# Two-layer graph transformer on one core: the 20-token tile's matrix products in one accumulating group instead of four column quarters

## The chip, the cores and the metric

The kernel runs on one core of a Trainium2 chip. The metric is the device time of one execution in microseconds (us). TensorE is called PE in the profile, and its weight loads PEld; VectorE is DVE, ScalarE is ACT, GpSimd is POOL, SyncE is SP.

## The reference, cut to what matters

A graph of 2708 tokens with 512 features goes through two transformer layers. Attention is restricted to the neighbours of each token (a random symmetric graph with self loops), so each row of the 2708 x 2708 score matrix has at most some twenty live entries. All arithmetic is fp32.

```python
q = (h @ Wq.T + bq); k = (h @ Wk.T + bk); v = (h @ Wv.T + bv)      # 8 heads of 64
scores = einsum('nhd,mhd->hnm', q, k) / 8, -1e9 where there is no edge
ctx = einsum('hnm,mhd->nhd', softmax(scores), v).reshape(n, 512)
h1 = layer_norm(h + ctx @ Wo.T + bo)
h2 = layer_norm(h1 + relu(h1 @ W1.T + b1) @ W2.T + b2)             # 512 -> 2048 -> 512
```

## The kernel before, in words

The tokens are sorted by their number of neighbours and cut into 22 tiles of 128 tokens. 2708 is 21 x 128 + 20, so the last tile, number 21, has 20 tokens; the diff's names for its size are `r` (rows of a tile) and `size(g)`.

**Stages.** First `first` computes keys and values of layer 0 for all tiles and makes the neighbour lists on DVE (lines 832 to 901); `first_queries` computes the queries, ranks the tokens by neighbours (`ranked`, line 756) and starts the attention (lines 903 to 959). Then each layer runs its tiles in eleven blocks of two. Attention of a tile gathers the rows of its neighbours' keys and values by indirect DMAs from POOL (`loads`, L1004) and works on DVE and ACT. The feed-forward part of a block works on PE and ACT; the attention of the coming blocks is spread beside it by hand (`advance`, `through`). The blocks are the same for both layers:

```python
blocks = [(20, 19), (18, 17), (7, 9), (6, 10), (5, 11), (0, 16)]
blocks += [(1, 15), (2, 14), (3, 13), (4, 12), (NT - 1, 8)]
```

so the 20-token tile is the first member of the last block in each layer. Its partner, tile 8, is full.

**Order.** The instructions of PE, ACT and SP are issued in the order in which the program text makes them; DVE's order is by hand in `first_queries` and at the start of layer 1, POOL's in layer 0; elsewhere a scheduler chooses the order of DVE and POOL when the program is built.

**The products.** `project(xs, r, wm, name)` (line 566) multiplies a tile's 512 features with a 512 x 512 matrix: four chunks of 128 features, each with the tokens as the stationary operand (128 x r) and 512 columns of the matrix streaming. In fp32 every such product is two LDWEIGHTS and two MATMUL instructions, so a projection is eight of each. For a full tile the four chunks accumulate into one PSUM tile `o[:r]` (L576). For the 20-token tile (`r <= Q4`, Q4 = 32) they go to four different quarters of the PSUM partitions, 0 to 19, 32 to 51, 64 to 83 and 96 to 115 (L571); the four partial sums are then added up: the reader that evacuates PSUM takes quarter 0, and `plus_rest` (line 583) adds quarters 1 to 3 with one DVE instruction each (L586, or L588 where a scale is needed).

**The feed-forward part** (`Layer.feed_forward`, line 1311) walks 16 chunks `f` of the hidden width: `pf` (L1351) multiplies W1 with the tokens of both tiles (128 + 20 = 148 columns in the last block), ACT applies relu into `ft` (L1359), and three chunks later `second(f)` multiplies W2 with `ft` into the PSUM accumulators `a0`, `a1` of the two tiles (L1324). For the 20-token tile `second` does nothing; instead `quarters(f)` (line 1333, L1339) handles four chunks at a time, each into its own quarter of the accumulator. The ends of both tiles follow: residual add (L1375, then `plus_rest`), layer norm (`norm`, L1147 to L1160, with one POOL instruction L1156), and in layer 1 an indirect DMA to the output from POOL (L1379). In layer 0, `keys_values` (line 1390) then computes keys and values of layer 1 for both tiles and scatters them to DRAM (L1417), before layer 1 can gather them.

The very end: a product with one column, `pr` (L1647), forms a flag that all checks held; each engine loads the flag (L1663) and branches past a fall-back path.

Of the kernel before, what the change touches and what calls it, by code (L numbers as in the profile page):

```python
# [13 lines left out]
ALU = mybir.AluOpType  # L14
# [5 lines left out]
DM = 512  # L20
# [11 lines left out]
SAFE = 60.0  # L32
LIST = 24
SEG = 247
Q4 = 32

CAPS = (22, 14, 13, 12, 12, 11, 11, 10, 10, 9, 9, 9, 9, 8, 8, 8, 7, 7, 7, 6, 5, 3)
SLOTS = 2
# [434 lines left out]
def by_edges(ctx: ExitStack, tc: tile.TileContext, x, xT, adj, layers, out, good):  # L473
# [92 lines left out]
    def project(xs, r, wm, name, other=False):  # L566

        o = (ps_f if other else ps).tile([P, DM], F32, tag="f" if other else "g", name=name)
        if r <= Q4:
            for c in range(NC):  # L570
                nc.tensor.matmul(  # L571
                    o[c * Q4 : c * Q4 + r], xs(c), wm[:, c, :], start=True, stop=True
                )
            return o
        for c in range(NC):
            nc.tensor.matmul(o[:r], xs(c), wm[:, c, :], start=(c == 0), stop=(c == NC - 1))  # L576
        return o

    def rest(o, r):

        return [o[q * Q4 : q * Q4 + r] for q in range(1, 4)] if r <= Q4 else []

    def plus_rest(to, o, r, scale=None):
        for part in rest(o, r):
            if scale is None:
                nc.vector.tensor_tensor(to, part, to, ALU.add)  # L586
            else:
                nc.vector.scalar_tensor_tensor(to, part, scale, to, ALU.mult, ALU.add)  # L588

    def finish(steps):  # L590
        for _ in steps:
# [240 lines left out]
    def first(w, meanwhile):  # L832

        xg = []

        def load():
            i = len(xg)
            b = i % XBS * XB
            bw = min(XB, N - b)
            t = wts.tile([P, NC, XB], F32, tag=f"w1_{5 + i % 3}", name="xg")  # L840
            xg.append(t)
            step = bw if i else P
            for a in range(0, bw, step):
                nc.sync.dma_start(
                    out=t[:, :, a : a + step], in_=chunked(xT)[:, :, b + a : b + a + step]
                )
                yield

        def tokens(t, again):

            i, c0 = t * P // XB, t * P % XB
            if c0 == 0 and len(xg) < 2 * XBS:
                finish(load())
            xs = xg[i + again * XBS]
            return lambda c: xs[:, c, c0 : c0 + size(t)]

        wk = wts.tile([P, NC, DM], F32, tag="wk", name="wk")
        halves = load()
        next(halves)
        for c in range(NC):  # L860
            nc.sync.dma_start(out=wk[:, c, :], in_=chunked(w["Wk"])[:, c, :])
            if c == 0:
                cols = [given_column(w, "bk")]
        cols.append(given_column(w, "bq"))
        finish(halves)
        turning = turned_row(cols[0], "bk", 1.0)
        bk = next(turning)
        wv = matrix(w, "Wv", "wv")
        pa = tc.tile_pool(name="pa", bufs=2)
        lists, counted, ranked, listed = lists_of(pa.__enter__())  # L870
        done, before = 0, None
        for t in range(NT):
            r = size(t)
            xs = tokens(t, 0)
            kv = wts.tile([P, 2 * DM], F32, tag=f"w2_{5 + t % 3}", name="kvs")
            k = project(xs, r, wk, "k")
            if t == 0:
                finish(turning)
            nc.vector.tensor_tensor(kv[:r, :DM], k[:r], bk[:r], ALU.add)
            plus_rest(kv[:r, :DM], k, r)  # L880
            v = project(xs, r, wv, "v", other=True)
            nc.scalar.copy(kv[:r, DM:], v[:r])
            plus_rest(kv[:r, DM:], v, r)
            if before:
                nc.scalar.dma_start(**before)
            before = dict(out=kv_d[0][t * P : t * P + r, :], in_=kv[:r])
            if t == 0:
                finish(load())
            while done < min(NT, 1 + LEAD * t):
                lists(done)  # L890
                done += 1
                if done == NT:
                    counts = counted()
            meanwhile(t)
            if t == QT:
                wq = matrix(w, "Wq", "wq")
                turning = turned_row(cols[1], "bq", DK**-0.5)
                bq = next(turning)
                finish(turning)
        nc.scalar.dma_start(**before)  # L900
        return bq, wq, counts, ranked, listed, pa, tokens

    def first_queries(bq, wq, counts, ranked, listed, pa, tokens, meanwhile):
# [14 lines left out]
        for t in range(NT):  # L918
# [10 lines left out]
            nc.vector.scalar_tensor_tensor(  # L929
                qs[:r, t % 2], q[:r], DK**-0.5, bq[:r], ALU.mult, ALU.add  # L930
            )
            plus_rest(qs[:r, t % 2], q, r, DK**-0.5)
            if t == OWN - 1:
                listed(True)
                pa.__exit__(None, None, None)
# [36 lines left out]
    def own_query(g, zT, to, bq, wq):  # L972
# [1 line left out]
        r = size(g)  # L974
        q = project(lambda c: zT[:, c, :r], r, wq, "q")
        nc.vector.scalar_tensor_tensor(to[:r], q[:r], DK**-0.5, bq[:r], ALU.mult, ALU.add)
        plus_rest(to[:r], q, r, DK**-0.5)

    def checked():

# [194 lines left out]
    class Layer:  # L1175
# [83 lines left out]
        def query(self, g, zT):  # L1259
# [4 lines left out]
            nc.vector.scalar_tensor_tensor(  # L1264
                qs[:r], q[:r], DK**-0.5, self.bq[:r], ALU.mult, ALU.add
            )
            plus_rest(qs[:r], q, r, DK**-0.5)
            self.kept()
            self.due = (g, qs)

# [7 lines left out]
        def attended(self, block, got):  # L1278
# [11 lines left out]
            for g, r, cT, xb in cTs:  # L1290
                o = project(lambda c: cT[:, c, :r], r, self.wo, "o")
                h = dn.tile([P, DM], F32, tag="h", name="h", bufs=4)
                nc.vector.tensor_tensor(h[:r], o[:r], xb[:r], ALU.add)
                plus_rest(h[:r], o, r)
                if self.n == 0:
                    nc.vector.tensor_tensor(h[:r], h[:r], self.bo[:r], ALU.add)
                norm(h, r, self.g1, self.e1b2)
# [13 lines left out]
        def feed_forward(self, block, hs, hT):  # L1311
# [5 lines left out]
            def second(f, only=None):  # L1317
                c0 = 0
                for g, a in zip(block, accs):
                    r = size(g)  # L1320
                    if only not in (None, g) or r <= Q4:
                        c0 += r
                        continue
                    nc.tensor.matmul(  # L1324
# [3 lines left out]
                        start=(f == 0),  # L1328
                        stop=(f == NFC - 1),
                    )  # L1330
                    c0 += r

            def quarters(f):
                c0 = 0
                for g, a in zip(block, accs):
                    r = size(g)
                    for i in range(f - 3, f + 1) if r <= Q4 else ():
                        q = i % 4 * Q4
                        nc.tensor.matmul(  # L1339
                            a[q : q + r],  # L1340
                            fts[i][:, c0 : c0 + r],
                            self.w2[i // 2][:, i % 2, :],
                            start=(i < 4),
                            stop=(i >= NFC - 4),
                        )
                    c0 += r

            for f in range(NFC):
# [11 lines left out]
                fts.append(ft)  # L1360
                if f >= LAG:
                    second(f - LAG)
                if f % 4 == 3 and f < NFC - 1:
                    quarters(f)
                yield None
            for g in block:
                for f in range(NFC - LAG, NFC):
                    second(f, g)
                    if g == block[-1] and f == NFC - LAG:
                        quarters(NFC - 1)  # L1370
            zs = []
            for g, a, h in zip(block, accs, hs):
                r = size(g)
                z = h
                nc.vector.tensor_tensor(z[:r], a[:r], h[:r], ALU.add)  # L1375
                plus_rest(z[:r], a, r)
                norm(z, r, self.g2, self.e2)
                if self.n == NL - 1:
                    nc.gpsimd.indirect_dma_start(  # L1379
# [10 lines left out]
        def keys_values(self, block, zs):  # L1390
# [12 lines left out]
            for i, (g, z, zT) in enumerate(zip(block, zs, zTs)):  # L1403
# [1 line left out]
                kv = kvs[:, i, :]  # L1405
                k = project(lambda c: zT[:, c, :r], r, self.kv[0], "k")
                nc.vector.tensor_tensor(kv[:r, :DM], k[:r], self.bk[:r], ALU.add)
                plus_rest(kv[:r, :DM], k, r)
                v = project(lambda c: zT[:, c, :r], r, self.kv[1], "v")
                nc.scalar.copy(kv[:r, DM:], v[:r])  # L1410
                plus_rest(kv[:r, DM:], v, r)
                nc.sync.dma_start(out=zT_d[n][g], in_=zT)
                nc.sync.dma_start(out=xb_d[n][g * P : g * P + r, :], in_=z[:r])
                yield
# [292 lines left out]
```

## Time and profile before

| | |
|---|---|
| times of three runs | 1941.27, 1941.85, 1946.15 us; median 1941.85 |
| the profiled execution | 1946.15 us; its span 1944.3 us, 1.85 us of it outside the span |
| PE busy | 1858.4 us (96%), mean granted clock 0.981 |
| DVE / ACT / POOL busy | 1321.0 (68%) / 934.7 (48%) / 809.3 us (42%) |
| L1339, the quartered W2 products | 64 MATMULs, 8.4 us of PE, 600 ns mean of one |
| L1324, the other W2 products | 1344 MATMULs, 632.2 us of PE, 596 ns mean of one |
| L571, the quartered projections | 8 projections of 8 MATMULs |
| L586 and L588, the rest of the quarters | 30 DVE instructions, some 0.685 us each |

PE's busy time is the time in which at least one matmul runs, and matmuls overlap: a group's busy time is less than its count times its mean. Groups of one line with different shapes are told apart by their shapes: "128*20" is a stationary operand with 20 columns. In a timeline, the bracket behind a row says how long the engine sat idle before it, and what it waited for; "issue" means nothing that the profile shows. In a table of windows the columns are the window, its length, the busy time of PE, PEld, DVE, ACT and POOL with the number of instructions, the granted PE clock, the DMA share and GB/s. The times of day in the text are us from the span's start.

### The profile page before, as it was taken

The numbers are of one execution on the slowest core, as the hardware profiler recorded it, in microseconds if no ns is written. First come the engines' busy times: TensorE is split into PE (matmuls) and PEld (weight loads), VectorE is DVE, ScalarE is ACT, GpSimd is POOL, SyncE is SP. The second block draws the span as 40 slices with busy tenths as digits, with TensorE's granted clock in tenths as the row PEclk, the third lists the DMA queues.
The fourth block names the chain that finished last, engine by engine and source line by source line (L and its number), as shares of the span: only waits on it lengthen the run. The fifth ranks groups of instructions, "written<-read, shape, count | busy, mean of one in ns | idle before, by whom it ended". The sixth has DMA issues, their size and how long they took to land. (4 is left out here: it accounts for less than half of the span.)

```text
span 1944.3 us, 20898 instructions
## 1 busy us (share of the span) xinstructions
PE 1858.4 (96%) x6162; PEld 1096.7 (56%) x6162; DVE 1321.0 (68%) x2172; ACT 934.7 (48%) x3219; POOL 809.3 (42%) x710
## 2 busy tenths in 40 slices
PE   9998968999999999999999997999999999999996
PEld 4443435556656556665665553566666666666663
DVE  5885467768759687695841237696987998877421
ACT  4660236445546655574451113555475767654510
POOL 3113526535536555364410124344555775546101
PEclk9999979999999999999999998999999999999998
DMA  9998848555646656554401478656665766643000
GB/s 322 355 314 299 275 136 302 172 179 184 205 138 201 217 188 197 177 183 154 146 17 65 136 246 325 202 197 204 203 222 168 251 222 220 209 155 125 17 6 14
DMA packets 131486, 366.92 MB, mean 189 GB/s; under 512 B 16668, under 2 KB 37004, under 8 KB 128654
## 3 DMA queue, kind: packets, MB, share of 16 engines
q0 software_dynamic: 69120, 246.35, 38.0%
q1 hardware_dynamic: 53332, 99.66, 14.8%
q10 hardware_dynamic: 8910, 19.48, 2.6%
q8 instruction: 50, 0.82, 0.2%
q14 instruction: 74, 0.61, 0.1%
HBM read 314.62 MB, written 50.83 MB: 188 GB/s over the span
## 5 line engine op out<-in xcount | busy, mean ns | idle before, releaser
L1004 POOL DMA_INDIRECT kv<-kv_d,idx x420 | 547.0, 1302 | 452.2 <-DVE acc L1080 273.5
L1351 PE MATMUL pf<-hT,w 128*128 128x256 f32 (+1 forms) x2816 | 637.2, 373 | 7.2 <-ACT ft L1359 5.2
L1324 PE MATMUL a<-w,ft 128*128 128x512 f32 x1344 | 632.2, 596 | 5.3 <-ACT ft L1359 4.4
L1351 PEld LDWEIGHTS pf<-hT,w 128*128 128x128 f32 x2816 | 521.2, 191 | 186.6 <-issue 106.5
L1359 ACT ACTIVATE ft<-pf,b 128x256 f32<-128x256 f32 (+1 forms) x352 | 160.3, 460 | 458.5 <-PE pf L1351 458.3
L1041 DVE TENSOR_TENSOR kv<-kv,q 128x1024 f32<-128x1024 f32 (+3 forms) x222 | 254.2, 1157 | 169.2 <-DMA kv<-kv_d,idx 131.1
L1324 PEld LDWEIGHTS a<-w,ft 128*128 128x128 f32 x1344 | 253.2, 191 | 198.6 <-issue 171.6
L1067 ACT ACTIVATE kv<-kv,p 128x64 f32<-128x64 f32 x1232 | 311.0, 335 | 5.0
L1047 DVE TENSOR_REDUCE sc<-kv 128x16 f32<-128x1024 f32 (+3 forms) x222 | 253.8, 1153 | 1.5
L1080 DVE TENSOR_TENSOR acc<-acc,kv 128x1024 f32<-128x1024 f32 (+2 forms) x178 | 204.0, 1146 | 18.9 <-ACT kv L1067 17.0
L1156 POOL TENSOR_TENSOR rd<-va,mhalf 128x1 f32<-128x1 f32 (+1 forms) x88 | 90.4, 1028 | 274.6 <-DVE va L1154 273.7
L576 PE MATMUL o<-wo,cT 128*128 128x512 f32 x336 | 151.1, 602 | 0.5 <-ACT cT L1171 0.5
L1073 DVE TENSOR_TENSOR kv<-kv,p 128x512 f32<-128x512 f32 (+1 forms) x178 | 121.4, 682 | 34.6 <-ACT p L1060 34.6
L1060 ACT ACTIVATE p<-sc,minus 128x8 f32<-128x8 f32 x420 | 102.8, 294 | 69.2 <-DVE sc L1047 62.1
L1111 ACT ACTIVATE cx<-acc,su 128x64 f32<-128x64 f32 (+1 forms) x352 | 88.5, 334 | 74.7 <-DVE su L1103 57.6
L576 PEld LDWEIGHTS o<-wo,cT 128*128 128x128 f32 x336 | 64.5, 193 | 83.2 <-issue 72.9
L681 ACT ACTIVATE code<-aj 128x2708 bf16<-128x2708 int32 (+1 forms) x22 | 73.3, 3332 | 49.2 <-POOL aj L677 49.0
L684 DVE MAX8 tops<-code 128x8 f32<-128x247 f32 (+2 forms) x242 | 83.1, 401 | 19.3 <-ACT code L681 19.3
L1160 DVE SCALAR_TENSOR_TENSOR h<-h,rd,ln_b 128x512 f32<-128x512 f32 (+1 forms) x88 | 65.6, 747 | 40.6 <-POOL rd L1156 40.6
L1067 ACT ACTIVATE acc<-kv,p 128x64 f32<-128x64 f32 (+1 forms) x352 | 88.8, 334 | 1.4
L1410 ACT COPY kvs<-v 128x512 f32<-128x512 f32 (+1 forms) x22 | 12.9, 586 | 158.9 <-PE v L576 138.5
L1375 DVE TENSOR_TENSOR h<-a,h 128x512 f32<-128x512 f32 (+1 forms) x44 | 29.9, 679 | 85.2 <-PE a L1339 48.8
(154 smaller groups left out, 1560.2 us busy)
## 6 DMA issues: line engine op xcount, KB each, us to landing
aj<-in_adj SPq DMA_DIRECT2D x21, 1354.0 KB, 8.4
kv_d<-kvs ACTq DMA_DIRECT2D x21, 512.0 KB, 7.4
w<-in_W SPq DMA_DIRECT2D x20, 512.0 KB, 6.5
xg<-in_xT SPq DMA_DIRECT2D x19, 512.0 KB, 8.6
kv<-kv_d,idx POOLq DMA_INDIRECT x420, 5.8
w<-in_W ACTq DMA_DIRECT2D x12, 512.0 KB, 7.2
q_d<-qs SPq DMA_DIRECT2D x22, 256.0 KB, 3.4
zT_d<-zT SPq DMA_DIRECT2D x22, 256.0 KB, 4.3
```

Of the source, the lines that this page charges most:

```text
L576: nc.tensor.matmul(o[:r], xs(c), wm[:, c, :], start=(c == 0), stop=(c == NC - 1))
L1004: nc.gpsimd.indirect_dma_start(out=to, out_offset=None, in_=table[:, :], in_offset=bass.IndirectOffsetOnAxis(ap=s, axis=0), bounds_check=N ...
L1041: nc.vector.tensor_tensor(kv[:r, :c, :DM], kv[:r, :c, :DM], self.q[:r].unsqueeze(1).to_broadcast([r, c, DM]), ALU.mult,)
L1047: nc.vector.tensor_reduce(self.sc[:r, s0 : s0 + c, :], kv[:r, :c, :DM].rearrange("p s (h d) -> p s h d", d=DK), AX.X, ALU.add,)
L1060: nc.scalar.activation(p[:r, s, :], self.sc[:r, s, :], AF.Exp, bias=minus[:r, g, s : s + 1])
L1067: nc.scalar.activation(to[:, i, hd], kv[:r, i, DM + h * DK : DM + (h + 1) * DK], AF.Copy, scale=p[:r, s0 + i, h : h + 1],)
L1073: nc.vector.tensor_tensor(to[:, 0, :].rearrange("p (h d) -> p h d", d=DK), kv[:r, 0, DM:].rearrange("p (h d) -> p h d", d=DK), p[:r, s0, : ...
L1080: nc.vector.tensor_tensor(self.acc[:r, :c, :], self.acc[:r, :c, :], kv[:r, :c, DM:], ALU.add)
L1156: nc.gpsimd.tensor_tensor(rd[:r], va[:r], mhalf[:r], ALU.pow)
L1324: nc.tensor.matmul(a[:r], fts[f][:, c0 : c0 + r], self.w2[f // 2][:, f % 2, :], start=(f == 0), stop=(f == NFC - 1),)
L1351: nc.tensor.matmul(pf[:, :w], self.w1[f // 2][:, c, f % 2 * P : f % 2 * P + P], hT[:, c, :w], start=(c == 0), stop=(c == NC - 1),)
L1359: nc.scalar.activation(ft[:, :w], pf[:, :w], AF.Relu, bias=self.b1[:, f : f + 1])
```

## The change

The quarters go. `project` treats every tile as a full one: four chunks accumulate into `o[:r]`. `second` no longer skips the 20-token tile, so that per chunk `f` PE now does the W1 products of the block, two MATMULs with a 20-column stationary operand for tile 21, and two with 128 columns for tile 8. `quarters`, `rest`, `plus_rest` and their calls are removed. Blocks, tile order and loads stay as they are.

```diff
-Q4 = 32
 ...
     def project(xs, r, wm, name, other=False):
         o = (ps_f if other else ps).tile([P, DM], F32, tag="f" if other else "g", name=name)
-        if r <= Q4:
-            for c in range(NC):
-                nc.tensor.matmul(
-                    o[c * Q4 : c * Q4 + r], xs(c), wm[:, c, :], start=True, stop=True
-                )
-            return o
         for c in range(NC):
             nc.tensor.matmul(o[:r], xs(c), wm[:, c, :], start=(c == 0), stop=(c == NC - 1))
         return o
-
-    def rest(o, r):
-        return [o[q * Q4 : q * Q4 + r] for q in range(1, 4)] if r <= Q4 else []
-
-    def plus_rest(to, o, r, scale=None):
-        for part in rest(o, r):
-            if scale is None:
-                nc.vector.tensor_tensor(to, part, to, ALU.add)
-            else:
-                nc.vector.scalar_tensor_tensor(to, part, scale, to, ALU.mult, ALU.add)
 ...
             nc.vector.tensor_tensor(kv[:r, :DM], k[:r], bk[:r], ALU.add)
-            plus_rest(kv[:r, :DM], k, r)
             v = project(xs, r, wv, "v", other=True)
             nc.scalar.copy(kv[:r, DM:], v[:r])
-            plus_rest(kv[:r, DM:], v, r)
 ...            (the same in first_queries, own_query, query, attended, keys_values)
                 for g, a in zip(block, accs):
                     r = size(g)
-                    if only not in (None, g) or r <= Q4:
+                    if only not in (None, g):
                         c0 += r
                         continue
                     nc.tensor.matmul(
 ...
-            def quarters(f):
-                c0 = 0
-                for g, a in zip(block, accs):
-                    r = size(g)
-                    for i in range(f - 3, f + 1) if r <= Q4 else ():
-                        q = i % 4 * Q4
-                        nc.tensor.matmul(
-                            a[q : q + r],
-                            fts[i][:, c0 : c0 + r],
-                            self.w2[i // 2][:, i % 2, :],
-                            start=(i < 4),
-                            stop=(i >= NFC - 4),
-                        )
-                    c0 += r
 ...
                 if f >= LAG:
                     second(f - LAG)
-                if f % 4 == 3 and f < NFC - 1:
-                    quarters(f)
                 yield None
             for g in block:
                 for f in range(NFC - LAG, NFC):
                     second(f, g)
-                    if g == block[-1] and f == NFC - LAG:
-                        quarters(NFC - 1)
 ...
                 nc.vector.tensor_tensor(z[:r], a[:r], h[:r], ALU.add)
-                plus_rest(z[:r], a, r)
                 norm(z, r, self.g2, self.e2)
```

## The prediction

> **What bounds the kernel now.** I read first the table of windows around the places where the 20-token tile is worked on, to see where more PE time is more time.
>
> ```profile
> 150.00:175.00 25.00, 18.88 (x54) 8.24 (x53) 19.95 (x60) 1.75 (x3) 2.73 (x4) 0.86 0.91 319
> 275.00:300.00 25.00, 20.82 (x74) 13.10 (x73) 19.96 (x31) 11.62 (x46) 6.68 (x7) 0.86 0.38 114
> 1050.00:1075.00 25.00, 25.00 (x94) 15.18 (x93) 8.56 (x17) 4.88 (x15) 2.83 (x3) 1.00 0.05 22
> 1100.00:1125.00 25.00, 25.00 (x96) 13.56 (x94) 2.25 (x4) 4.41 (x13) 2.00 (x2) 1.00 0.80 258
> 1900.00:1925.00 25.00, 25.00 (x132) 15.23 (x131) 1.10 (x2) 4.22 (x11) 0.00 (x0) 1.00 0.00 1
> ```
>
> Both last blocks (1088 to 1137 and 1890 to 1926) run with PE busy for 25.00 of 25 us at clock 1.00, and DVE, ACT and POOL nearly idle: PE alone sets the time there, and nothing covers an added matmul. The first two rows are the other case: at the first keys and queries PE has idle time, and its clock fell (0.86).
>
> Next the timeline of weight loads in the last block, which prices the quarters.
>
> ```profile
> 1901.60 0.32 PEld L1324 LDWEIGHTS a<-w,ft 128*128 128x128 f32 x2
> 1902.16 0.19 PEld L1351 LDWEIGHTS pf<-hT,w 128*128 128x128 f32 x1 [0.24 <-issue]
> 1902.59 0.94 PEld L1351 LDWEIGHTS pf<-hT,w 128*128 128x128 f32 x7 [0.24 <-issue]
> 1903.47 0.32 PEld L1324 LDWEIGHTS a<-w,ft 128*128 128x128 f32 x2
> 1904.54 0.14 PEld L1339 LDWEIGHTS a<-w,ft 128*20 128x20 f32 x8 [0.76 <-issue]
> 1905.53 1.05 PEld L1351 LDWEIGHTS pf<-hT,w 128*128 128x128 f32 x8 [0.85 <-issue]
> 1906.52 0.32 PEld L1324 LDWEIGHTS a<-w,ft 128*128 128x128 f32 x2
> ...
> 1924.64 0.19 PEld L1324 LDWEIGHTS a<-w,ft 128*128 128x128 f32 x1 [0.24 <-issue]
> 1925.59 0.09 PEld L1647 LDWEIGHTS pr<-held,ones 128*1 128x1 f32 x2 [0.76 <-issue]
> ```
>
> A chunk without quarters takes 1903.47 - 1901.60 = 1.87 us, one with them 1906.52 - 1903.47 = 3.05: a group of eight quartered MATMULs (four chunks) costs 1.18. A 512-column MATMUL has a pitch of 0.43 us here (1902.59 - 1902.16). Eight in quarters are two passes of four side by side, 0.86; the other 0.32 is entering and leaving: the load before them waits 0.76 instead of 0.24, and the one behind them 0.85. The last row matters most: L1647 has no quarters, only a stationary operand of one column, and its load also waits 0.76. So what stalls PE is the change between wide and narrow operands, not the quartering.
>
> **The change part by part.** All differences are against this profile.
>
> W2 products of tile 21, per layer. Removed: 4 groups x 1.18 = 4.7 us. Added: 16 chunks x 2 = 32 MATMULs x 0.43 = 13.8. Per chunk they now stand between the W1 products and tile 8's, all 128 wide: one entry and exit for each of the 13 chunks in the loop and one for the last three together, 14 x 0.32 = 4.5. Net 13.8 + 4.5 - 4.7 = 13.6, for two layers **+27.2**. Bounds: with no stall for an uncrowded narrow operand 13.8 - 4.7 = 9.1 per layer; I take 0.32, because the L1647 row shows the stall. Nothing hides this.
>
> Projections. Each was 1.18 and becomes 8 x 0.43 + 0.32 = 3.76, +2.58. The two `o` projections (1064.2, 1868) lie in saturated PE: **+5.2**. The layer 1 query (1384.8) too, but PE later waits 2.0 and 0.6 us near 1632 and 1638, so 0 to 2.6; attention's ACT steps are queued behind the relu steps that PE feeds, so most of it carries on: **+1.8**. The keys and values between the layers are one quartered stretch from 1146.02 to 1147.94 = 1.92; they become 16 x 0.43 + 0.32 = 7.2, +5.3. They stand ahead of tile 8's keys and values, whose scatter (1156.05) the first gather of layer 1 waits for (1159.64), so it all counts, less 0.4 that tile 8's `v` now waits for `plus_rest` to free PSUM (load at 1151.44, idle 0.62 rather than 0.24): **+4.9**. The shorter layer norm ahead of it brings nothing: the two query projections that cover it keep PE busy to 1144.7.
>
> The first keys and values (154.2): PE then waits for DVE:
>
> ```profile
> 162.20 6.43 PE L576 MATMUL q<-wq,xg 128*128 128x512 f32 x8 [6.07 <-DVE kvs L879]
> 168.47 0.61 PE L763 MATMUL pr<-hot,tri 128*128 128x264 f32 x2
> ```
>
> Their +5.3 fits into the 6.07, at no cost; the PSUM that PE waits for isn't freed by the removed adds. But this idle time is also why the eight MATMULs after it run at half clock, 5.8 us from load to load where 3.5 is full speed. With 0.8 us of idle left the clock should hold (after a gap of 1.03 us at 1190 the pitch stayed 0.43), and the ranking behind them (L763, then 22 scatters on POOL, then the gathers, on which PE waits 14 us before 263) starts 2.3 earlier: **-2.3**, bounds 0 and -2.4. If the cover weren't there it would cost 5.3. The first query of tile 21 (276.2) goes into an idle 3.66 before 285.2, at no cost; that idle also halves the clock, and 32 MATMULs take 9.03 instead of 32 x 0.215 = 6.9: 0 to -2.1 there, mostly lost in PE's next waits for attention (1.97 and 2.86 us at 315 and 323): **-0.7**.
>
> DVE loses 30 instructions x 0.685 = 20.5 us. 27 of them lie beside saturated PE or in DVE's own waits: no gain, except that at 1384 DVE is nearly as full as PE (24.45 of 25), which is why the query's price above can fall to 0. The last three are in the tail, with POOL's scatters to the output behind them:
>
> ```profile
> 1929.21 2.18 POOL L1156 TENSOR_TENSOR rd<-va,mhalf 20x1 f32<-20x1 f32 x2 [32.06 <-DVE va L1154]
> 1931.96 1.16 POOL L1379 DMA_INDIRECT out<-h,ident_i  x1 [0.57 <-DVE h L1160]
> 1936.58 1.01 POOL L1379 DMA_INDIRECT out<-h,ident_i  x1 [3.47 <-issue]
> ```
>
> PE's last W2 MATMUL ends at 1925.66. Both norms run interleaved, tile 21's scatter starts 6.3 us later, and tile 8's waits until the first has landed (4.6 from start to start), though its rows were ready at 1932.3. In the new order tile 21's sums end 6 x 0.43 + 0.2 = 2.8 before tile 8's, and the add, statistics, POOL step and two scalings (0.69 + 0.69 + 0.3 + 1.3 + 0.75 = 3.7) let its scatter start some 1.3 after the end of PE instead of 6.3. The second follows 4.6 after, at 5.9 instead of 10.9: **-5.0**. The order of DVE and POOL is a scheduler's, so -2 (tile 21's last scaling behind all of tile 8's first steps) to -6.
>
> Sum: 27.2 + 5.2 + 1.8 + 4.9 - 2.3 - 0.7 - 5.0 = **+31.1**. The profiled execution (span 1944.3, 1946.15 in all) would become 1977.2; the median of the runs shown lies 4.3 lower, 1941.85, and becomes 1973.
>
> [...]
>
> **The rivals.**
> (a) No stall. If a lone 20-column operand at partition 0 counts as a full one, each term loses its 0.32s: W2 +18.2, `o` +4.5, query +1.5, transition +4.6, with the same early and late gains: 28.8 - 8.0 = +20.8, 1963. For: the quarters were the only 20-column products. Against: L1647, whose load is no quarter and waits as long. Chance 0.13.
> (b) No gains at the ends: clock, attention chain and scheduler give nothing back but 2 us of tail, and the query counts in full: 27.2 + 5.2 + 2.6 + 5.3 - 2 = +38.3, 1980. For: DMA is 0.8 to 0.9 busy at 150 to 250, so an earlier ranking may only wait for its gathers. Against: the gap of 0.8. Chance 0.17.
> (c) Faster. The added MATMULs are covered, as the first keys are, and the 20.5 us of DVE and the tail remain: -2.3 - 0.7 - 5.0 = -8, 1934. It needs some 31 us of PE idle in the two last blocks and the transition (it decides from there on); the windows show 25.00 of 25, and 24.83 at 1125. Chance 0.03.
> That the change doesn't do what its name says: the blocks are already in this order, and the diff moves none; only the quarters go, as costed.
>
> **How the numbers follow.** The forecast, 1973, has 0.67. The range takes in (a) at its low side with an early gain of 4 (1961) and (b) with a full-price transition (1980): 1961 to 1980. A measurement of this kernel tells 0.3%, some 6 us, from no change. Faster by more needs (c): 0.02. Within it: 0.02. Slower: 0.96.
>
> **What would show it.** In the new profile the "128*20" rows of L1324 should stand alone in pairs, each entered by a load that waited about 0.76, with a chunk of 1.87 + 0.86 + 0.32 = 3.05 us each time instead of every fourth time, and the last blocks 13.6 us longer. PE at 162 should run at a pitch of 0.43, and the two last scatters lie 1 and 6 us after PE's end. A chunk of 2.73 would be rival (a); a ranking that starts earlier with gathers that don't, rival (b). Idle PE inside the last blocks would make the whole sum wrong.

## The result, and the profile after

The changed kernel takes 1972.57 us (median of 4 runs, 1969.74 to 1974.75) where the kernel before, run beside it, takes 1943.05 (4 runs, 1941.27 to 1946.15): a ratio of 1.0149, 95% interval 1.013 to 1.0169, or 29.5 us slower. Run once more beside another set of runs of before (below), it took 1972.87 against 1941.06: ratio 1.0161, interval 1.0146 to 1.0176, 31.8 us slower. The forecast was 1973.0, from a sum of +31.1.

Its profiled execution took 1974.75 us, span 1972.9, mean granted clock 0.989 (before: 1946.15, 1944.3, 0.981). PE is busy for 1896.1 us, 37.7 more than before; DVE for 1302.7, 18.3 less. The table of windows at the places that the prediction used (the last one moved along with the last block; columns: window, length, busy us of PE, PEld, DVE, ACT, POOL with the number of instructions, granted clock, DMA share, GB/s):

```profile
150.00:175.00 25.00, 24.01 (x60) 9.53 (x60) 16.27 (x55) 1.16 (x2) 4.32 (x6) 1.00 0.92 309
275.00:300.00 25.00, 23.15 (x84) 14.64 (x83) 17.78 (x29) 15.89 (x62) 10.81 (x11) 1.00 0.55 171
1050.00:1075.00 25.00, 25.00 (x84) 13.93 (x83) 7.48 (x14) 4.18 (x13) 1.87 (x2) 1.00 0.00 0
1100.00:1125.00 25.00, 25.00 (x80) 11.93 (x79) 2.25 (x4) 2.70 (x6) 2.00 (x2) 1.00 0.76 246
1925.00:1950.00 25.00, 25.00 (x101) 12.61 (x99) 0.00 (x0) 3.43 (x9) 0.00 (x0) 1.00 0.00 1
```

The last blocks are still 25.00 of 25 for PE at clock 1.00, so nothing covered the added products. In the last row PE issues 101 matmuls in 25 us instead of 132. Over the whole kernel both versions issue 6162; tile 21's no longer run side by side in quarters (where a group of eight took 1.05 us before, at 1904.54), so the same number takes longer. At 150 and 275 PE's idle time is mostly filled and the clock is 1.00 where it was 0.86.

The timeline of weight loads in the last block of layer 1, from one chunk's load for tile 8 to the next:

```profile
1932.26 0.30 PEld L1300 LDWEIGHTS a<-w,ft 128*128 128x128 f32 x2 [0.85 <-issue]
1932.80 0.19 PEld L1312 LDWEIGHTS pf<-hT,w 128*128 128x128 f32 x1 [0.24 <-issue]
1933.23 0.94 PEld L1312 LDWEIGHTS pf<-hT,w 128*128 128x128 f32 x7 [0.24 <-issue]
1934.32 0.12 PEld L1300 LDWEIGHTS a<-w,ft 128*20 128x20 f32 x2 [0.15 <-issue]
1935.29 0.30 PEld L1300 LDWEIGHTS a<-w,ft 128*128 128x128 f32 x2 [0.85 <-issue]
```

From one load for tile 8 to the next, 1935.29 - 1932.26 = 3.03 us, in every chunk of the loop; before, it was 1.87 in three of four and 3.05 in the fourth. The pair of tile 21 (128*20) stands alone between W1's products and tile 8's. The load behind it waits 0.85, the one into it only 0.15.

The timeline of PE at the first query projection, and POOL's rows at the very end:

```profile
162.73 3.70 PE L569 MATMUL q<-wq,xg 128*128 128x512 f32 x8 [0.94 <-DVE kvs L861]
166.27 0.61 PE L745 MATMUL pr<-hot,tri 128*128 128x264 f32 x2
```

```profile
1959.24 0.93 POOL L1134 TENSOR_TENSOR rd<-va,mhalf 20x1 f32<-20x1 f32 x1 [40.97 <-DVE va L1132]
1961.27 0.95 POOL L1335 DMA_INDIRECT out<-h,ident_i  x1 [1.10 <-DVE h L1138]
1962.84 0.92 POOL L1134 TENSOR_TENSOR rd<-va,mhalf 128x1 f32<-128x1 f32 x1 [0.62 <-DVE va L1132]
1964.84 1.03 POOL L1335 DMA_INDIRECT out<-h,ident_i  x1 [1.08 <-DVE h L1138]
```

The idle time ahead of the query fell from 6.07 to 0.94, and its eight MATMULs now take 3.54 us from the first to the ranking's first (166.27 - 162.73; before 6.27). At the end, the last W2 MATMUL ends at 1960.04; the two scatters start 1.23 and 4.80 us later (before: 6.3 and 10.9), and the second now waits for its own rows on DVE, not for the first to land.

**Where the 28.6 us of the two spans lie.** I set the starts of the same PE rows in both traces side by side; each line is the growth of one stretch.

| stretch | before | after | difference |
|---|---|---|---|
| start to the block before the last of layer 0 (its first `pf`) | 1012.42 | 1005.16 | -7.3 |
| that block, with `o` of the last block beside it | 76.20 | 78.75 | +2.55 |
| last block, layer 0: first `pf` to the first query of layer 1 | 49.19 | 62.44 | +13.25 |
| from there to tile 8's keys | 10.14 | 14.88 | +4.7 |
| tile 8's keys to block 2 of layer 1 | 227.55 | 229.49 | +1.9 |
| block 2 of layer 1, with tile 21's query | 68.43 | 70.98 | +2.55 |
| blocks 3 to 8 of layer 1 | 385.40 | 386.20 | +0.8 |
| block 9, with `o` of the last block beside it | 61.59 | 64.14 | +2.55 |
| last block, layer 1: first `pf` to the last MATMUL's end | 34.74 | 48.00 | +13.25 |
| tail: from there to the end of the span | 18.67 | 12.89 | -5.8 |

Those that lie in saturated PE, and the tail, come to 2.55 + 13.25 + 4.7 + 2.55 + 2.55 + 13.25 - 5.8 = +33.05 us, 33.1 before rounding. The remaining three (-7.3, +1.9, +0.8) are -4.6 in this execution, and they are the ones that differ from kernel to kernel: block 1 of layer 1 (part of the +1.9 row), which no edit here touches, takes 71.9 us before and 74.0 in the kernel below whose only edit is at the very end. The first row differs as much where its code is the same: 1012.42 before, and 1008.39, 1013.26 and 1007.33 in the three kernels below that keep it as it was (independent scatters, W2 alone, early quarters). With the early products plain it is 1005.16 here and 1001.49 to 1006.68 in four more traces. So it is shorter after the change, by 5.8 us on average, but the 7.3 of one pair of executions is not its size.

### The profile page after: what moved, and what is told of

It reads as the page before. It is cut to its first block, busy times and chain, and to the rows that moved or that the text cites. A ratio compares the mean times of both kernels' runs of the same rounds, so it can differ in the third digit from the quotient of the medians.

```text
span 1972.9 us, 20865 instructions
## 1 busy us (share of the span) xinstructions
PE 1896.1 (96%) x6162; PEld 1103.9 (56%) x6162; DVE 1302.7 (66%) x2142; ACT 933.7 (47%) x3219; POOL 816.1 (41%) x710
## 5 line engine op out<-in xcount | busy, mean ns | idle before, releaser
L982 POOL DMA_INDIRECT kv<-kv_d,idx x420 | 556.6, 1325 | 446.3 <-DVE acc L1058 267.2
L1300 PE MATMUL a<-w,ft 128*128 128x512 f32 (+1 forms) x1408 | 661.9, 595 | 10.5 <-ACT ft L1320 7.5
L1300 PEld LDWEIGHTS a<-w,ft 128*128 128x128 f32 (+1 forms) x1408 | 255.7, 186 | 231.1 <-issue 196.2
L1058 DVE TENSOR_TENSOR acc<-acc,kv 128x1024 f32<-128x1024 f32 (+2 forms) x178 | 204.0, 1146 | 18.3 <-ACT kv L1045 16.3
L569 PE MATMUL o<-wo,cT 128*128 128x512 f32 (+1 forms) x352 | 157.4, 600 | 0.5 <-ACT cT L1149 0.5
L1051 DVE TENSOR_TENSOR kv<-kv,p 128x512 f32<-128x512 f32 (+1 forms) x178 | 121.5, 683 | 35.2 <-ACT p L1038 35.2
L569 PEld LDWEIGHTS o<-wo,cT 128*128 128x128 f32 (+1 forms) x352 | 65.9, 189 | 88.0 <-issue 77.5
L1371 POOL DMA_INDIRECT kv_d<-kvs,ident_i x22 | 24.7, 1121 | 157.6 <-ACT kvs L1365 78.3
```

Of the source, the lines that this page charges most:

```text
L982: nc.gpsimd.indirect_dma_start(out=to, out_offset=None, in_=table[:, :], in_offset=bass.IndirectOffsetOnAxis(ap=s, axis=0), bounds_check=N ...
L1051: nc.vector.tensor_tensor(to[:, 0, :].rearrange("p (h d) -> p h d", d=DK), kv[:r, 0, DM:].rearrange("p (h d) -> p h d", d=DK), p[:r, s0, : ...
L1058: nc.vector.tensor_tensor(self.acc[:r, :c, :], self.acc[:r, :c, :], kv[:r, :c, DM:], ALU.add)
L1300: nc.tensor.matmul(a[:r], fts[f][:, c0 : c0 + r], self.w2[f // 2][:, f % 2, :], start=(f == 0), stop=(f == NFC - 1),)
```

## Experiments

Two of the changed kernel's traits are on trial first, the price of a width change and the early gain; then the tail, then whether the terms add up, and last a version that might beat both. Stretches and tails below are measured as in the table above.

**The width change: tile 21's W2 products with a stationary operand of 128 columns.** The MATMULs are as many and as long, but no operand is narrow (the rows beyond the 20 tokens are never read).

```diff
-                        a[:r],
-                        fts[f][:, c0 : c0 + r],
+                        a,
+                        fts[f][:, c0 : c0 + P],
```

> The changed kernel, but tile 21's W2 products load all 128 columns that lie in ft (its own 20 and the first 108 of tile 8's, whose rows of the sum nobody reads): as many MATMULs of as many columns, none of them narrow. Theory (entering and leaving narrow operands stalls PE): a chunk of the last block falls from 3.03 to 2.73 us (1.87 + 2 x 0.43), the 14 changes per layer at some 0.3 go, 4.2 us per layer and 8.5 in all: about 21 us above the kernel before, 1964. Rival (streaming the 32 more MATMULs is the whole price, the waiting loads are only drawn that way): a chunk stays at 3.03 and the time at 29 above, 1972. Second rival (the wider load costs more than the narrow one saves): above 1972.

Measured: 1969.19 us, ratio to before 1.0125 (1.0101 to 1.0149), by the medians 23.0 us above before where 21 was expected; single runs spread from 1960.05 to 1973.02, so the blocks are the sharper measure. The two last blocks take 58.18 and 43.74, 4.25 less in each than after the change. The timeline of its weight loads:

```profile
1916.19 0.32 PEld L1300 LDWEIGHTS a<-w,ft 128*128 128x128 f32 x2
1916.74 0.19 PEld L1300 LDWEIGHTS a<-w,ft 128*128 128x128 f32 x1 [0.24 <-issue]
1917.17 0.19 PEld L1300 LDWEIGHTS a<-w,ft 128*128 128x128 f32 x1 [0.24 <-issue]
1917.60 0.19 PEld L1312 LDWEIGHTS pf<-hT,w 128*128 128x128 f32 x1 [0.24 <-issue]
...
1918.91 0.32 PEld L1300 LDWEIGHTS a<-w,ft 128*128 128x128 f32 x2
```

No load in the loop waits longer than 0.24, and a chunk takes 2.72 us, 0.31 less than with the narrow pair. A matmul on 128 columns of which 108 are thrown away is cheaper here than one on 20. 4.25 / 14 = 0.304 us for each entry with its exit.

**The same, by number of changes: tile 21's W2 products gathered in groups of four chunks,** in one accumulating group, so that each layer has 4 entries instead of 14.

```diff
-                    if only not in (None, g):
+                    if only not in (None, g) or r < P:
...
+                if f % 4 == 3 and f < NFC - 1:
+                    fours(f)        # four chunks' pairs of tile 21 in a row, into a[:r]
```

> The changed kernel, but tile 21's W2 products wait for four chunks and then run as eight narrow MATMULs in a row into one group, where the quarters stood: 4 changes of width per layer instead of 14. Theory (stall per change): 10 x 0.3 x 2 = 6 us below the changed kernel, about 23 above the kernel before, 1966, with one chunk in four at 1.87 + 3.44 + 0.3 = 5.6 us and the others at 1.87. Rival (price per MATMUL): 29 above, 1972.

Measured: 1967.77 us, ratio 1.0115 (1.0079 to 1.0152); the last blocks take 59.40 and 44.95, 3.05 less in each, which is 10 x 0.305. Its weight loads around a group (five equal rows left out):

```profile
1922.89 0.32 PEld L1300 LDWEIGHTS a<-w,ft 128*128 128x128 f32 x2
1923.96 0.12 PEld L1313 LDWEIGHTS a<-w,ft 128*20 128x20 f32 x2 [0.76 <-issue]
1924.41 0.10 PEld L1313 LDWEIGHTS a<-w,ft 128*20 128x20 f32 x1 [0.33 <-issue]
...
1927.50 1.05 PEld L1324 LDWEIGHTS pf<-hT,w 128*128 128x128 f32 x8 [0.85 <-issue]
```

Two different edits give the same price, 0.304 and 0.305, each by the number of changes that it takes away. Within the group the narrow loads follow each other at the ordinary pitch of 0.43: it is the change that costs, not the narrow operand.

**The clock gap alone: the kernel before, with 12 MATMULs that nobody reads in the 6.07 us ahead of the first query.** Quarters and adds all stay.

```diff
+            if t == NT - 1:
+                o = ps_f.tile([P, DM], F32, tag="f", name="warm")
+                for c in range(6):
+                    nc.tensor.matmul(o[:r], xs(c % NC), wv[:, c % NC, :], start=True, stop=True)
```

> The kernel before with its quarters, its rests and all its sums, and twelve idle MATMULs (20 columns wide, a result that nobody reads) put behind tile 21's first values, where PE stood idle for 6.07 us. Theory (the idle gap halved the clock of what follows): the first query's eight MATMULs run at a pitch of 0.43 instead of 0.85, the ranking starts about 2.3 us earlier, and with later waits that it shortens the whole is 2 to 5 us below the kernel before, 1938 to 1941. Rival (the changed kernel's early gain came from the removed DVE instructions): the pitch is 0.43, but the ranking's first scatter and the time stay as they were, 1943.

Measured: 1942.19 us, ratio 0.9994 (0.9972 to 1.0016). PE there:

```profile
154.99 5.31 PE L887 MATMUL warm<-wv,xg 128*20 128x512 f32 x12
160.24 3.70 PE L576 MATMUL q<-wq,xg 128*128 128x512 f32 x8
163.78 0.61 PE L763 MATMUL pr<-hot,tri 128*128 128x264 f32 x2
```

The query's eight MATMULs take 3.54 us instead of 6.27 with nothing changed but the idle time ahead of them, so that idle time is what had slowed them. The ranking's scatters start at 167.92 instead of 171.85, so the rival's sign, scatters that stay where they were, did not come. What this is worth at the end of the kernel (4.0 us less by the medians, 0.06% by the ratio), the interval can tell neither from nothing nor from the 2 to 5 us that were expected.

**The clock gap by the change itself: the kernel before, only tile 21's first keys and values out of the quarters,** with their six adds on DVE gone.

```diff
-            k = project(xs, r, wk, "k")
+            k = project(xs, r, wk, "k", plain=True)
...
-            plus_rest(kv[:r, :DM], k, r)
-            v = project(xs, r, wv, "v", other=True)
+            v = project(xs, r, wv, "v", other=True, plain=True)
...
-            plus_rest(kv[:r, DM:], v, r)
```

> The kernel before, with only tile 21's first keys and values (layer 0) in one accumulating group and without their rests; all else in quarters. Theory (clock): as with idle MATMULs in the gap, the ranking 2.3 us earlier, 2 to 5 us below the kernel before, and the same as that run within 1 us. Rival (the six removed DVE instructions count): 2 to 4 us below the run with idle MATMULs. Second rival (5.3 us more of PE reach the end, no cover): 1948.

Measured: 1944.19 us, ratio 0.9994 (0.9977 to 1.0012). From its timeline of PE:

```profile
161.60 3.70 PE L576 MATMUL q<-wq,xg 128*128 128x512 f32 x8
165.14 0.61 PE L763 MATMUL pr<-hot,tri 128*128 128x264 f32 x2
...
208.28 4.60 PE L576 MATMUL q<-wq,xg 128*128 128x512 f32 x5 [3.43 <-DMA xg<-in_xT]
```

The first pitch is as in the fill (3.54 us), and the ranking's scatters start at 168.53. Then PE waits 3.43 us at 208 for a load of token features, which in the profiled execution of before had come in time, and the first feed-forward block starts 4.1 later than before. A wait for that load also stands in the traces of the wide variant (1.36 us), of the groups of four (1.60) and of two kernels below (1.56 and 3.65), one of which still has the quarters there; in others it is absent. The time lies level with the fill's by the ratio and 2.0 us above it by the medians, so the rival's 2 to 4 below it, for the six adds, isn't borne out; nor is the second rival's 5 us over before, a ratio of 1.0026. So an early start can be lost to a transfer, and whether it is differs between kernels of equal code at that place.

**The early gain in the whole change: the changed kernel again, beside a variant that keeps the quarters of layer 0's first keys, values and query.** The variant is the changed kernel with the quarters' branch of `project` and `plus_rest` back for those three calls.

```diff
-    def project(xs, r, wm, name, other=False):
+    def project(xs, r, wm, name, other=False, plain=False):    # plain=True in all later calls
+        if r <= Q4 and not plain:                             # quarters, as before
...
+            plus_rest(kv[:r, :DM], k, r)
+            plus_rest(kv[:r, DM:], v, r)
+            plus_rest(qs[:r, t % 2], q, r, DK**-0.5)
```

> The changed kernel once more, unaltered, beside a variant that keeps the quarters at the beginning alone. What is open: the profiled execution of the changed kernel had 7.3 us of early gain (everything up to 1060 us came that much earlier) where the forecast had 3.0. Its stretches that lie in saturated PE, and its tail, add up to 26.6 + 5.0 + 2.6 + 4.6 - 5.8 = +33.0 us; what the time stays below that is the early gain. Theory of the forecast: an early gain of about 3, ratio 1.0154. Rival, 7.3 is what the change brings every time: ratio 1.0132. Third, no early gain that lasts: ratio 1.0170.

> The changed kernel, but with the quarters (and their adds) kept for the 20-token tile's first keys, values and query of layer 0, which lie beside idle PE. It pays all of the price, +33.0 us, and has none of what an early plain projection can bring: ratio to before 1.0170 by the theory that the clock gap at the first queries gives something, with the changed kernel 3 us below it (forecast) or 7.3 us below it (the profiled execution). Rival: what is gained there is lost in the waits for the gathers; then both variants take the same time to within 1.5 us, and any spread at 200 to 300 us is one of transfers that varies from execution to execution.

Measured, side by side: the changed kernel 1972.87 us (1971.99 to 1975.41), ratio 1.0161 (1.0146 to 1.0176); with the early quarters 1976.27 (1974.08 to 1980.04), ratio 1.0186 (1.017 to 1.0202). The difference of the medians is 3.4 us, near the forecast's 3.0, but the two intervals overlap. The rival of 7.3 every time (ratio 1.0132) lies below the changed kernel's interval here, though just inside that of the first comparison (1.013 to 1.0169). The third, no gain that lasts (1.0170), lies inside the interval here, and two variants at most 1.5 us apart aren't excluded either. With the early quarters the kernel stands 35.2 above before, where the fixed terms made 33; that is the lower end of its interval. The two profiled executions don't show where the 3.4 lie: at the start of block 2 of layer 0 they stand at 444.04 and 444.65.

**The tail: the changed kernel with tile 8's three last chunks ahead of tile 21's.**

```diff
-            for g in block:
+            for g in reversed(block) if w < 2 * P else block:
                 for f in range(NFC - LAG, NFC):
                     second(f, g)
```

> The changed kernel with one order turned round: in the last block the three products that are left over at the end come first for tile 8, then for tile 21. PE's work is the same. Theory (the tail became shorter because tile 21's sums end 2.8 us before PE's end, so that its norm runs beside PE): now tile 21's chain starts at PE's end, its scatter to the output starts some 4.0 us after that end instead of 1.2, the second scatter 7.5 to 8.6 after, and the time from PE's end to the span's end is 15.6 to 16.7 us instead of 12.9. Rival (only the three removed additions shortened the tail): it stays at 12.9, give or take 0.7.

Measured, in one run: 1977.54 us, tail 17.91 us (1957.80 to 1975.71). POOL at its end:

```profile
1960.24 2.18 POOL L1134 TENSOR_TENSOR rd<-va,mhalf 20x1 f32<-20x1 f32 x2 [44.02 <-DVE va L1132]
1963.00 1.16 POOL L1335 DMA_INDIRECT out<-h,ident_i  x1 [0.58 <-DVE h L1138]
1967.95 1.00 POOL L1335 DMA_INDIRECT out<-h,ident_i  x1 [3.80 <-issue]
```

The direction is the theory's, the size is beyond it (15.6 to 16.7 expected): with both sums ready at nearly the same time, the two norms run interleaved again (POOL's two steps stand in one row, "x2"), as before the change, so the first scatter starts 5.2 after PE's end, and the second waits for it. 17.91 - 12.89 = 5.0 us of the 5.8 is the order of the two sums, and 18.67 - 17.91 = 0.8 is left for the three adds. That rest isn't shown: two kernels that keep the adds and the old order (the first keys and values alone, the later fills alone) have tails of 17.96 and 17.70.

**The wait between the two last scatters: the kernel before, with the two scatters to the output declared independent** (they write different tokens' rows).

```diff
+                    tc.declare_no_dep(put.ins, group="put", reason="every token has one place")
+                    tc.add_to_no_dep_group("put", put.ins)
```

> The kernel before, with the two last scatters to the output (tile 21, then tile 8, different rows) declared independent of each other, so that POOL doesn't wait for the first to land before it starts the second. Theory: that landing is what the second scatter waited for (its rows were ready at the first one's start), so it starts 7.5 to 8 us after PE's end instead of 10.9, and the time from PE's end to the span's end falls from 18.7 to 15.3-15.8 us. Rival: it waited for something else on POOL or in the queue, and nothing moves: 18.7.

Measured, in one run: 1940.02 us, tail 15.55 us (1922.73 to 1938.28).

```profile
1929.03 1.15 POOL L1379 DMA_INDIRECT out<-h,ident_i  x1 [0.57 <-DVE h L1160]
1930.49 1.00 POOL L1379 DMA_INDIRECT out<-h,ident_i  x1 [0.30 <-issue]
```

The second starts 7.76 after PE's end, the idle time ahead of it is 0.30 instead of 3.47, and the tail is 3.1 shorter: the second scatter had waited for the first to land.

**W2 alone: the kernel before, with only tile 21's W2 products out of the quarters.** All its projections stay quartered.

```diff
-                    if only not in (None, g) or r <= Q4:
+                    if only not in (None, g):
...
-                    quarters(f)
...
-                        quarters(NFC - 1)
...
-                plus_rest(z[:r], a, r)
```

> The kernel before with only the W2 products of tile 21 taken out of the quarters (and with them their three residual adds per layer); all projections stay quartered. What is put on trial is whether the terms of the sum add up, and how much the early gain is worth. Theory: the last block of each layer grows by the 13.3 us that the trace after showed (49.2 to 62.5 and 34.7 to 48.0), the tail falls to 12.9 as after, so the profiled span lies 26.6 - 5.8 = 20.8 us above that of before, apart from the scatter of the first 1000 us. Against the changed kernel, the projections (2 x 2.5 for o, 2.55 for the query, 4.6 for keys and values, 12.2 in all) are missing and so is the early gain G that came with plain first keys and values: ratio to before 1.0107 in any case; the changed kernel's 1.0149 stands above it by 12.2 - G, that is 8.2 us with G = 4. Rival: the early gain is worth all of the 7.3 us that the profiled execution showed; then the two kernels lie only 4.9 us apart and the ratio here is 1.0124 or more. Third: there is no early gain at all: 12.2 us apart, ratio 1.0086 or less.

Measured: 1966.57 us, ratio 1.0121 (1.0092 to 1.015). In its trace the last blocks take 62.45 and 48.01 and the tail 12.72, as in the full change; the stretches with `o` grow by 0.0 in both layers, and the one with tile 21's query by -0.1. So the terms are separate and add up where PE is saturated. On the early gain the run is no judge: its interval holds the theory's 1.0107 and the rival's 1.0124, and misses only the third (1.0086), and by little.

**Filling three gaps and freeing the tail: the kernel before with its quarters,** the fill at the first query, the independent scatters, and 13 and 6 calls of a product that nobody reads in PE's gaps of 14.2 us (layer 0) and 7.4 us (layer 1) ahead of `o`; and, to tell its parts apart, the two later fills by themselves.

```diff
                 flip(cx, r, cT[:, :, :r], self.bv)
+                if g == order[0]:
+                    o = ps_f.tile([P, DM], F32, tag="f", name="warm")
+                    for c in range((13, 6)[self.n]):
+                        nc.tensor.matmul(o, ones, self.wo[:, c % NC, :], start=True, stop=True)
```

> A version meant to beat the kernel before: its quarters all stay, the two last scatters are independent, and PE's idle time is filled with products that nobody reads at three places (six calls in the 6.07 us gap at the first queries, 13 calls in the 14.2 us gap of layer 0 between the two transpositions of block 0's attended, 6 in the 7.4 us gap of layer 1), so that the clock isn't halved behind them. Theory: -3.3 in the tail, -5 where the clock stays full behind the two later gaps (o and the first W1 products of a layer at a pitch of 0.43 instead of 0.85), 0 to -3 from the first gap: -8 to -11, ratio 0.995 to 0.996. Rival (what is gained early and in the middle is lost in the next wait for a transfer, as the ranking's gain was): only the tail stays, ratio 0.998. Third: the filling delays the products behind it, and the ratio is 1.000 or above.

> The kernel before with PE's two gaps of 14.2 us (layer 0) and 7.4 us (layer 1), both between the two transpositions of block 0's attended, filled with 13 and 6 products that nobody reads, and nothing else; it tells which part of the combined version brought its 4.6 us. Theory: the pieces add up, 3.1 of the 4.6 is the tail, so this one is 1.5 us or a little more under before, ratio 0.998 to 0.9992, and in the profile the transpositions and o products behind the gap have a clock of 1.00. Rival: the fills are worth the 5 us that the half-clock stretches suggest, and the fill at the first queries costs something: ratio 0.9975 or less. Third: they bring nothing (the next wait, for the attention, swallows it): ratio 1.000.

Measured: all together 1938.35 us (1935.23 to 1944.35, 12 runs), ratio 0.9978 (0.9962 to 0.9994); the later fills alone 1941.14, ratio 0.9995 (0.9981 to 1.0009). The timeline of PE, first in the combined version and then in that with the later fills alone:

```profile
248.85 11.32 PE L1293 MATMUL warm<-wo,ones 128*128 128x512 f32 x26
262.87 1.91 PE L1170 MATMUL tp<-ident,cx 128*128 128x128 f32 x4 [2.69 <-ACT cx L1115]
264.57 5.95 PE L576 MATMUL q<-wq,xg 128*128 128x512 f32 x8
```

```profile
249.18 11.32 PE L1289 MATMUL warm<-wo,ones 128*128 128x512 f32 x26
264.64 1.91 PE L1166 MATMUL tp<-ident,cx 128*128 128x128 f32 x4 [4.14 <-ACT cx L1111]
266.34 5.93 PE L576 MATMUL q<-wq,xg 128*128 128x512 f32 x8
```

In layer 0 the fill missed its aim: it ends 2.69 and 4.14 us before the next product is ready, and the transpositions behind it still take 1.91 us and the eight query MATMULs 5.9 (at a pitch of 0.43 they take 3.5). In layer 1 it left 2.43 us in the combined version, where the clock fell, and 2.19 in the one with the later fills alone, where it held: from the second transposition to the block's first W1 product that one takes 18.33 us instead of 21.04 before. Even so its time can be told neither from no gain nor from the 1.5 us expected; the rival's ratio of 0.9975 is out. The combined version's gain of 4.6 us (1942.91 - 1938.35) is not far from the tail's 3.1, and the rival, "only the tail stays", names its ratio; where the rest of it comes from isn't shown. It is the only kernel here that is faster than both, by a fifth of a per cent, and its quarters all stay.

## Why the prediction was right, and where its terms were off

The forecast (1973.0, slower) held: 1972.57 in the first runs, 1972.87 in the second. That the times agree to 0.4 us is partly luck: the kernel before came out at 1943.05 beside the change, not at the 1941.85 from which the forecast starts, and the growth is 29.5 where 31.1 was forecast. Rival (a) needed a chunk of 2.73; it is 3.03, and 2.72 only with the wide operand. Rival (b)'s 1980 lies outside all runs of the changed kernel, although its mechanism, a gain lost to a transfer, does occur, and its full price for the query is what came. Rival (c) needed idle PE in the last blocks; there is none.

- **W2 products**, forecast +27.2: measured 13.25 + 13.25 = +26.5. The change costs 0.304 where 0.32 stood, which over 14 is 0.2 per layer. The step held: the stall was read from a one-column product without quarters, and the wide variant shows that it is the width. The price, 0.30 us for a 20-column pair between wide operands, also holds where the narrow operand starts at partition 0 and nothing is packed; what PE does in that time is not shown.
- **Where PE stalls**, forecast "each entered by a load that waited about 0.76": wrong for the chunks in the loop. The load into the narrow pair waits 0.15 behind W1's 148-column MATMULs, and the one behind the pair 0.85 instead of none. In the group of four chunks, which stands behind 512-column MATMULs, the entry does wait 0.76. The wait of a single load thus depends on its neighbours, and only the length of the whole chunk gives the price.
- **The two `o` projections**, forecast +5.2: +2.55 each, 5.1. **Keys and values between the layers**, forecast +4.9: +4.7.
- **Layer 1's query**, forecast +1.8 in bounds of 0 to 2.6: the upper bound is what came, +2.55 (and -0.1 in the W2-only kernel, which keeps this quarter). PE's later waits gave nothing back: blocks 3 to 8, in which they lie, take 384.84 to 386.56 us in the six traces with this query plain and 385.01 to 386.55 in the seven that keep its quarter. The term was mis-sized by 0.75: a wait further on was taken for a credit without a row that showed its releaser to be independent of PE.
- **The tail**, forecast -5.0: -5.8. The mechanism held; the turned order gives 5.0 back in its one run. The first scatter came where it was put (1.23 against 1.3 after PE's end). The second came at 4.80 and not 5.9, as in the separated order it no longer waits 4.6 for the first: it starts 3.57 after it, when its rows are ready.
- **The early terms**, forecast -2.3 and -0.7: the step from gap to clock to ranking is shown (the fill alone makes the eight MATMULs take 3.54 us). The value is known only roughly. The two profiled executions put 7.3 on the first stretch, and 5.7 in that of the repeated run, with equal code differing by up to 5.9 there; the medians with and without the early quarters give 3.4, and the two comparisons with before, by the medians, leave 33.1 - 29.5 = 3.6 and 33.1 - 31.8 = 1.3. So the forecast -3.0 lies among the measured values, which run from 1.3 to the 5.8 of the traces' average, and one pair of profiled executions by itself would have misled. What stays open is through which wait the gain reaches the end: the first keys and values alone, on the kernel before, and the fill (ratio 0.9994 each) can be told neither from nothing nor from 3 us.

The forecast's sum is 31.1; the fixed stretches of the table with 3.4 of early gain give 33.1 - 3.4 = 29.7, and the two comparisons 29.5 and 31.8. Its parts missed by -0.7 (W2), +0.75 (query), -0.8 (tail) and less; the errors partly cancel.

## What to carry to other kernels

Where PE is saturated, an operand of 20 columns cost as much streaming time here as one of 128 (a pitch of 0.43 us for a 512-column MATMUL with either), plus 0.30 us for the change of width, in and out together: pack it four-fold (eight MATMULs for 1.18 us here, change included), or gather it so that fewer changes are made, or leave it wide. Price an edit in the stretches where PE is full, which agree to 0.1 us between kernels; take a gain ahead of the first blocks from medians with and without it and not from one profiled execution. At the end of a kernel look at which tile's sums end first: finishing one tile some 2.8 us ahead of the other was worth 5.0 us here with the same work on PE.

## What the runs showed of the hardware that was not expected

PE's clock can fall after idle times much shorter than the 6 us ahead of the first query, and need not: the first row is of before (eight 256-column MATMULs; the group ahead of it took 1.99 us), the second of after (eight 512-column MATMULs, which take 3.7 us at full clock).

```profile
317.34 3.26 PE L1351 MATMUL pf<-hT,w 128*128 128x256 f32 x8 [1.97 <-ACT ft L1359]
```

```profile
1652.41 3.70 PE L1300 MATMUL a<-w,ft 128*128 128x512 f32 x8 [2.80 <-ACT ft L1320]
```

A wait of 1.97 us slowed what followed, one of 2.80 did not, and the 2.69 us behind the fill above did. The clock records of these traces show half speed (a granted clock of 0.50) only in stretches of 3.413 us or a multiple of it (up to 13.65 in before and after), apart from the one that the end of the kernel cuts. Within a trace all of them start on one grid of that length: before, at 160.90, 253.06, 283.78 and 317.92, which are 27, 9 and 10 steps apart.

That grid settles it. Divided along their own grids from 60 us on, the 13 traces have 7003 windows at full speed. Each of the 98 with more than 2.02 us of idle PE was followed by half speed, none of the 6886 with less than 1.84 was, and of the 19 between, 9 were. Before and after alone have 1078 of these windows: 16 with more than 2.02 us, all followed by half speed, 1059 with less than 1.84, none, and 3 between (1.97, 2.00 and 2.00), of which two were. The wait of 1.97 us lies whole in one window (314.50 to 317.92), and the clock fell at its end. The 2.80 are split by the line at 1650.76 into 1.16 and 1.64, and it held. Of the 2.69 behind the fill, 2.29 lie ahead of the line at 262.46, and it fell. So what counted in these traces was not the length of a gap but how much idle time fell into one window, and where the lines lie differs from execution to execution (after's at 251.30 is 26.5 steps from before's at 160.90). That would explain why kernels with the same code over a stretch in layer 0 or at the start of layer 1 differ by some 2 us there; it was not tried.

The other surprise is the wide operand: 128 columns, most of them unused, are 0.31 us per chunk cheaper than 20 (2.72 against 3.03).
